# Attention softmax totals: one transfer from SBUF to SBUF instead of a pass through DRAM, and earlier places for the reciprocal and the division

## The chip, the cores and the metric

The kernel runs on one core of a Trainium2 chip. The metric is the time on the device in microseconds (us) of one execution. A core has five engines that run side by side: PE (TensorE, matrix products), DVE (VectorE), ACT (ScalarE), POOL (GpSimd) and SP (SyncE), which in this kernel does nothing but issue transfers. An engine carries out its instructions strictly in the order in which they stand in its queue. If one of them waits, all that stand behind it on that engine wait too. This holds for SP's queue of transfers as well.

## The reference

For four batches of 1024 tokens of width 1024 (float32) the reference computes, cut to what matters:

```
xn  = rms_norm(x) * (1 + scale(emb)) + shift(emb)
q, k, v = split(xn @ W_qkv)              # 16 heads of 64
q, k = rms_norm(q), rms_norm(k)
attn = softmax(q @ k.T / 8)              # 1024 x 1024 for each of 4 x 16 heads
o    = attn @ v
x1   = x + o + o @ W_out
out  = x1 + causal_conv(x1, w = cond, 4 taps) + b
```

The change touches the last step of the softmax: the totals of `exp(...)` over the keys, their reciprocals, and the multiplication of `attn @ v` by them.

## The kernel before, in words

**Units.** The attention of a batch is done for pairs of heads, and for each pair in two halves of 512 queries. That makes 4 x 8 x 2 = 64 units, numbered here 0 to 63 in order of time; units 0 to 15 belong to batch 0. The loop at the end of the kernel makes one turn for each unit p. In turn p TensorE computes the scores of unit p (`scores`, L688) in between the products `attn @ v` of unit p - 1 (`values`, L751, into the one PSUM tile `pav`), then the totals of unit p - 1 (`finish`, L766), and then a long stretch of other products: the projections to q, k and v for later heads (`pqkv`, L648, by a Strassen scheme of seven products), the output projection (`po`, L940 and L1009) and transposes.

**The softmax of a unit.** ScalarE copies the scores to SBUF (L696), VectorE takes a running maximum (`mx`, L705), GpSimd reduces it over the partitions (`mb`, L710), ScalarE copies it to PSUM (`mbp`, L719). Then VectorE subtracts it from eight score tiles (the shifts, L724), ScalarE takes the exponentials (L728) and GpSimd adds them up (`sum`, L730, seven additions one after the other). In the next turn the ones-matrix product L766 adds `sum` over the partitions: the totals.

**The chain from the totals to the division.** `spread` (L784) copies the totals from PSUM to `tots`, where the 4 x 256 totals (two heads, two halves of the queries) lie on partitions 0, 32, 64 and 96. Four transfers write them to DRAM (`scrT`, L787), one reads them back as a tile of 128 partitions by 8 (`few`, L789). `invert` takes the reciprocal of this tile on VectorE (L792), writes it to DRAM (`scrR`, L794) and reads it back twice as broadcast (`rec`, two transfers, L797). `divide` multiplies `pav` by `rec` on VectorE (`oT`, L806) and stores the result (`scrO`, L810). `pav` has one buffer, so the first product of the next unit's `values` waits until `oT` has read it.

**What sets the order.** The orders of PE, DVE, ACT and POOL are written out by hand, by a planner in the kernel. It keeps a clock of its own, in planned microseconds, which is moved by the work that it gives to TensorE (`tick`). `defer(delay, key, step)` puts a step on a list with the due time clock + delay, and at each `tick` all steps that are due are issued in the order of their due times; equal due times go in the order in which they were put on the list. `finish` defers `spread` by 0.2 and `invert` by 8.0. Two `tick`s of 0.9 later `softmax` defers the maximum by 2.6, a filler by 2.7, the shifts by 7.6 + 1.8 per tile (1.6 in batch 0), and the loop defers `divide` by `DIVIDE` = 18.0. The filler (`fill_gap`) issues work on VectorE that has no fixed time: the scaling of q and k (`qk`, L498) and the combinations of weights and of sums (L565, L868, L894). The order of SP's queue is not written by hand: the tile framework places each transfer by its own reckoning of when it can start.

Of the kernel before, what the change touches and what calls it, by code (L numbers as in the profile page):

```python
# [10 lines left out]
F32 = mybir.dt.float32  # L11
# [4 lines left out]
P = 128  # L16
# [5 lines left out]
def kernel(  # L22
# [32 lines left out]
    nc = tc.nc  # L55
# [12 lines left out]
    QN = N // 4  # L68
# [10 lines left out]
    dram = ctx.enter_context(tc.tile_pool(name="dram", bufs=1, space=bass.MemoryType.DRAM))  # L79
# [16 lines left out]
    def defer(delay, key, step):  # L96
        pending.append((clock[0] + delay, next(serial), key, step))
# [10 lines left out]
    def tick(us):  # L108

        clock[0] += us  # L110
        flush(lambda e: e[0] <= clock[0])
# [565 lines left out]
    class Unit:  # L677
# [82 lines left out]
        def finish(self):  # L760
            b, c = self.pr.b, self.pr.c
            tot = ps_m.tile([P, HN], F32, tag="m", name=f"tot_{self.name}")
            for g in range(4):
                h, i = divmod(g, 2)
                some = slice(0, HN) if (b, c) == (B - 1, NJ - 1) else slice(i * QN, (i + 1) * QN)
                nc.tensor.matmul(  # L766
                    tot[32 * g : 32 * (g + 1), : some.stop - some.start],
                    ones,
                    self.sum[:, h, some],
                    start=True,  # L770
                    stop=True,
                )
            tick(2 * PAIR)
            self.tot = tot
            if (b, c) == (B - 1, NJ - 1):
                return
            key = ("tot", self.name)
            defer(0.2, key, lambda: self.spread(tot))
            defer(8.0, key, self.invert)

        def spread(self, tot):

            sums = apool.tile([P, HN], F32, tag="rec", name=f"tots_{self.name}", bufs=1)
            nc.scalar.copy(sums[:, :QN], tot[:, :QN])  # L784
            scr = dram.tile([4, QN], F32, tag=f"tot_{self.name}", name=f"scrT_{self.name}")
            for g in range(4):
                nc.sync.dma_start(scr[g : g + 1, :], sums[32 * g : 32 * g + 1, :QN])  # L787
            self.few = small.tile([P, 2 * HN // P], F32, tag="few", name=f"few_{self.name}", bufs=1)
            nc.sync.dma_start(self.few, scr.rearrange("g (p i) -> (g p) i", p=32))  # L789

        def invert(self):
            nc.vector.reciprocal(self.few, self.few)  # L792
# [280 lines left out]
    SHARES = (0.25, 0.5, 0.25)  # L1073
    LEADS = ((11, 7), (10, 9))
    LEADS_LAST = ((11, 7), (10, 12))
    DIVIDE = 18.0
    STEP_FIRST = 1.6
    BEHIND_FIRST = 22.0
    LATER = ((0, 0), (4, 0))
# [243 lines left out]
    for p in range(B * NB):  # L1323
# [10 lines left out]
        def fill():  # L1334
            run(next(stretches))
# [19 lines left out]
        if last is not None:  # L1355
            defer(2.7 if p > B * NB - 2 else DIVIDE, ("oT", last.pr.b, last.pr.c, last.half), last.divide)
        fill()
# [47 lines left out]
```

## Time and profile before

| | |
|---|---|
| median of 3 runs (2842.89, 2851.01, 2853.53) | 2851.01 us |
| the profiled execution, its own time | 2850.32 us |
| its span, first to last instruction | 2848.5 us |
| busy: PE, DVE, ACT, POOL | 97%, 76%, 54%, 46% |
| PE busy from 160 to 800 us of the span (batch 0) | 605.80 of 640 us |
| PE busy from 800 to 2640 us | 1832.53 of 1840 us |
| PE busy from 2640 us to the end | 191.43 of 209 us |
| mean granted TensorE clock | 0.993 |
| mean busy share of the DMA engines, 160 to 800 us, 800 to 2640 us | 0.52, 0.55 |

A line of the page's list of waits reads: engine and line of the waiting instruction, `<-` what ended its wait, then the total in us, the number of times and the longest. A line of the timeline reads: start in us, length in us, engine, line, operation, tiles `out<-in`, shape, the number of instructions merged, and in brackets the idle time of the engine just before them and what ended it.

### The profile page before, as it was taken

The page shows a single profiled execution, that of the slowest core. Times are in us where ns is not written, and L with a number is a line of the kernel's source. Part 1 is how long each engine was busy: PE and PEld are TensorE (multiplying, and loading weights), DVE is VectorE, ACT ScalarE, POOL GpSimd, SP SyncE. Part 2 cuts the span into 40 slices and gives each one's busy share as a digit, 9 for nine tenths or more (in the row PEclk, how much of TensorE's full clock was granted, in tenths as well). Part 3 has the DMA queues.
Part 4 walks back from the last instruction along what each step waited for, and adds up shares of the span by engine and source line. Part 5 has one row for each costly group of instructions (what it writes and reads, how often), then busy time and mean ns, then how long its engine had stood idle before and what let it go on. Part 6 is the DMA issues. An engine that isn't in the chain of part 4 may idle for free.

```text
span 2848.5 us, 32001 instructions
## 1 busy us (share of the span) xinstructions
PE 2764.3 (97%) x10581; PEld 1315.6 (46%) x10581; DVE 2162.1 (76%) x2579; ACT 1541.5 (54%) x2221; POOL 1323.4 (46%) x534
## 2 busy tenths in 40 slices
PE   6999999999999999999999999999999999999998
PEld 3544444444444445444444445444444444444344
DVE  4578788877888777788777777788778867787863
ACT  4255666655555566655555556565455545555532
POOL 2055554455554454353555355354455445544520
PEclk9999999999999999999999999999999999999999
DMA  9854555645554556674565556665565444533334
GB/s 318 276 170 145 192 174 187 204 152 172 174 196 158 175 192 209 208 234 161 165 208 180 169 180 212 193 228 182 166 214 197 144 135 165 167 104 105 114 108 118
DMA packets 416844, 509.40 MB, mean 179 GB/s; under 512 B 40816, under 2 KB 326824, under 8 KB 406952
## 3 DMA queue, kind: packets, MB, share of 16 engines
q1 hardware_dynamic: 416680, 507.36, 54.6%
q8 instruction: 85, 1.39, 0.2%
q14 instruction: 79, 0.65, 0.1%
HBM read 411.85 MB, written 95.40 MB: 178 GB/s over the span
## 4 chain that ended last, share of the span: by engine, by line
PE 79%; DVE 11%; DMA 4%; ACT 2%; issue 2%; SPq 1%; POOL 0%; DVEq 0%; ACTq 0%; POOLq 0%
PE pqkv_P L648 31%; PE pav L751 16%; PE s L688 15%; PE po L1009 5%; PE po_P L940 5%; DVE mx L705 4%; PE po L940 4%; DVE sp L724 2%; PE qkt L506 1%; DVE qk L498 1%; DMA rec<-scrR 1%; ACT sp L696 1%; PE po L995 1%; PE tot L766 1%; DMA we<-in_L_cond_W_emb_dram 1%
## 5 line engine op out<-in xcount | busy, mean ns | idle before, releaser
L648 PE MATMUL pqkv_P<-w_P,a 128*128 128x384 f32 x3456 | 1177.5, 492 | 18.2 <-issue 6.6
L730 POOL TENSOR_TENSOR sum<-sum,sp 128x1024 f32<-128x1024 f32 x384 | 934.7, 2434 | 35.9 <-ACT sp L728 4.8
L648 PEld LDWEIGHTS pqkv_P<-w_P,a 128*128 128x128 f32 x3456 | 642.4, 191 | 482.7 <-issue 77.7
L696 ACT COPY sp<-s 128x1024 f32<-128x1024 f32 x512 | 501.2, 1017 | 500.1 <-PE s L688 500.0
L728 ACT ACTIVATE sp<-sp 128x1024 f32<-128x1024 f32 x512 | 531.9, 1055 | 221.3 <-DVE sp L724 217.6
L724 DVE TENSOR_TENSOR sp<-sp,mbp 128x1024 f32<-128x1024 f32 x512 | 603.5, 1209 | 21.4 <-ACT mbp L719 21.2
L710 POOL PARTITION_ALL_REDUCE mb<-mx x64 | 219.7, 3432 | 849.7 <-DVE mx L705 421.3
L705 DVE TENSOR_TENSOR mx<-mx,sp 128x1024 f32<-128x1024 f32 x384 | 486.3, 1266 | 133.2 <-ACT sp L696 103.6
L688 PE MATMUL s<-qT,kT 64*128 64x512 f32 x2048 | 509.0, 615 | 2.0 <-ACT sp L696 2.0
L751 PE MATMUL pav<-sp,v 128*64 128x512 f32 x2048 | 484.5, 605 | 17.4 <-DVE oT L806 17.1
L730 POOL TENSOR_TENSOR sum<-sp,sp 128x1024 f32<-128x1024 f32 x64 | 151.5, 2366 | 486.7 <-ACT sp L728 186.5
L688 PEld LDWEIGHTS s<-qT,kT 64*128 64x128 f32 x2048 | 175.6, 185 | 306.3 <-issue 137.6
L751 PEld LDWEIGHTS pav<-sp,v 128*64 128x64 f32 x2048 | 131.6, 137 | 334.5 <-issue 287.4
L1045 DVE SCALAR_TENSOR_TENSOR y<-x,cols,y 128x512 f32<-128x512 f32 x192 | 241.7, 1263 | 48.0 <-ACT y L1033 43.4
L705 DVE TENSOR_TENSOR mx<-sp,sp 128x1024 f32<-128x1024 f32 x64 | 105.2, 1644 | 138.2 <-ACT sp L696 138.2
L667 DVE TENSOR_TENSOR qk<-u,pqkv_P 128x256 f32<-128x256 f32 x256 | 105.7, 413 | 74.0 <-PE pqkv_P L648 73.2
L1009 PE MATMUL po<-ob,wo 128*128 128x512 f32 x352 | 155.4, 593 | 0.5 <-DVE wo L989 0.5
L940 PE MATMUL po_P<-o_P,wq_P 128*128 128x512 f32 x320 | 143.9, 592 | 0.8 <-DMA o_P<-scrS 0.8
L498 DVE TENSOR_TENSOR qk<-qk,ms 128x1024 f32<-128x1024 f32 x64 | 136.0, 2145 | 0.0
L719 ACT COPY mbp<-mb 128x1024 f32<-128x1024 f32 x64 | 65.1, 1017 | 105.6 <-POOL mb L710 105.3
L940 PE MATMUL po<-o_P,wq_P 128*128 128x512 f32 x240 | 108.0, 592 | 0.0
L485 ACT ACTIVATE sq<-qk 128x512 f32<-128x512 f32 x128 | 76.8, 628 | 55.1 <-DVE qk L667 55.1
(94 smaller groups left out, 1753.0 us busy)
## 6 DMA issues: line engine op xcount, KB each, us to landing
a<-scrA SPq DMA_DIRECT2D x212, 512.0 KB
w_P<-scrB SPq DMA_DIRECT2D x64, 768.0 KB
o_P<-scrS SPq DMA_DIRECT2D x40, 1024.0 KB
w_P<-in_L_cond_W_qkv_dram SPq DMA_DIRECT2D x192, 192.0 KB
o_P<-scrO SPq DMA_DIRECT2D x30, 1024.0 KB
scrA<-r SPq DMA_DIRECT2D x28, 896.0 KB
wq_P<-scrW SPq DMA_DIRECT2D x70, 256.0 KB
xc<-in_x_dram SPq DMA_DIRECT2D x64, 256.0 KB
```

The lines of the kernel that those rows point to most:

```text
L648: nc.tensor.matmul(pm, (chunk.r(place) if a is None else a[:, k, :])[:, t % 2 * P : (t % 2 + 1) * P], w[:, k, :], start=(k == 0), stop=(k ...
L688: nc.tensor.matmul(ps[:, h, :], pr.kT[kt // HT][h * D : (h + 1) * D, kt % HT * P : (kt % HT + 1) * P], pr.qT[self.half][h * D : (h + 1) * ...
L696: nc.scalar.copy(sp, ps)
L705: nc.vector.tensor_max(self.mx, self.mx if kt > 1 else self.sp[0], self.sp[kt])
L710: nc.gpsimd.partition_all_reduce(self.mb.rearrange("p h q -> p (h q)"), self.mx.rearrange("p h q -> p (h q)"), P, bass_isa.ReduceOp.max,)
L724: nc.vector.tensor_sub(self.sp[kt], self.sp[kt], self.mb)
L728: nc.scalar.activation(sp, sp, AF.Exp)
L730: nc.gpsimd.tensor_tensor(self.sum, self.sum if kt > 1 else self.sp[0], sp, ALU.add)
L751: nc.tensor.matmul(self.pav[h * D : (h + 1) * D, :], self.pr.v[kt // HT][:, kt % HT, h * D : (h + 1) * D], self.sp[kt][:, h, :], start=(kt ...
L940: nc.tensor.matmul(pm, self.w[name][:, k, :], self.o[name][:, k, :], start=(k == 0 and name not in ("P2", "P3", "P4")), stop=(k == KH - 1),)
L1009: nc.tensor.matmul(self.pm, self.w[kh][:, k % KH, :], oTs[b, k, half], start=False, stop=(k == NJ - 1),)
L1045: nc.vector.scalar_tensor_tensor(self.y, self.x1[:, k : k + HN], cols[:, r : r + 1], self.y, ALU.mult, ALU.add)
```

## The change

The totals go from `tots` to `few` by one transfer of SP that reads four partitions of SBUF and writes 128; the tile `scrT` in DRAM and its four transfers are gone. The delay of `invert` goes from 8.0 to 4.5 planned microseconds, and `DIVIDE` from 18.0 to 12.0. Every unit from 0 to 61 goes through this code. The last two take the reciprocal of the whole totals on VectorE (L804), and the division of unit 62 has a delay of its own.

```diff
             key = ("tot", self.name)
             defer(0.2, key, lambda: self.spread(tot))
-            defer(8.0, key, self.invert)
+            defer(4.5, key, self.invert)
 
         def spread(self, tot):
 
             sums = apool.tile([P, HN], F32, tag="rec", name=f"tots_{self.name}", bufs=1)
             nc.scalar.copy(sums[:, :QN], tot[:, :QN])
-            scr = dram.tile([4, QN], F32, tag=f"tot_{self.name}", name=f"scrT_{self.name}")
-            for g in range(4):
-                nc.sync.dma_start(scr[g : g + 1, :], sums[32 * g : 32 * g + 1, :QN])
             self.few = small.tile([P, 2 * HN // P], F32, tag="few", name=f"few_{self.name}", bufs=1)
-            nc.sync.dma_start(self.few, scr.rearrange("g (p i) -> (g p) i", p=32))
+            nc.sync.dma_start(self.few, sums[0:P:32, :QN].rearrange("g (p i) -> g p i", p=32))
...
-    DIVIDE = 18.0
+    DIVIDE = 12.0
```

## The prediction

> **What bounds the kernel now.** First the windows by stage: PE is busy 1832.53 of 1840 us between 800 and 2640 us, so the change cannot win more than 7.5 us there. The room is in batch 0 (160 to 800 us, 34.2 us idle) and at the end (from 2640 us). Next the list of waits, for what the changed chain costs, on PE, on DVE and in SP's queue:
>
> ```profile
> PE pav L751 <- DVE oT L806: 17.1, 10, 5.1
> ...
> DVE oT L806 <- DMA rec<-scrR: 44.8, 24, 4.2
> ...
> DVE few L792 <- DMA few<-scrT: 11.7, 8, 1.7
> ...
> SPq L787 <- ACT tots L784: 827.3, 61, 18.3
> ...
> SPq L797 <- DMA scrR<-few: 89.7, 41, 4.0
> ```
>
> PE waits ten times for a division. VectorE waits 24 times for `rec`, but only PE's time counts. The timeline of unit 13's division, one of the ten, shows why:
>
> ```profile
> 672.48 0.38 ACT L784 COPY tots<-tot 128x256 f32<-128x256 f32 x1
> ...
> 672.88 1.12 SPq L787 DMA_DIRECT2D scrT<-tots  x4
> 674.87 0.34 SPq L789 DMA_DIRECT2D few<-scrT  x1
> ...
> 682.73 1.03 SPq L794 DMA_DIRECT2D scrR<-few  x1
> ...
> 688.14 1.13 SPq L797 DMA_DIRECT2D rec<-scrR  x2
> ...
> 681.80 0.20 DVE L792 RECIPROCAL few<-few 128x8 f32<-128x8 f32 x1
> ...
> 685.19 2.34 DVE L724 TENSOR_TENSOR sp<-sp,mbp 128x1024 f32<-128x1024 f32 x2
> ...
> 693.52 0.69 DVE L806 TENSOR_TENSOR oT<-pav,rec 128x512 f32<-128x512 f32 x1 [1.54 <-DMA rec<-scrR]
> ...
> 694.27 5.35 PE L751 MATMUL pav<-sp,v 128*64 128x512 f32 x16 [2.14 <-DVE oT L806]
> ```
>
> From here times count from the end of the `tots` copy (672.86 here). `few` is asked for at 2.0, but its reciprocal stands in VectorE's queue behind other work, until 8.9. `scrR` is issued at 9.9, `rec` at 15.3, and the division starts at 20.7, after seven shifts; PE was ready at 19.3. The 16 products after that wait take 5.35 us, against 3.65 us after unit 1's wait of 1.55 us: the profile has the granted clock at half for 3.4 us from 695.0.
>
> **The change part by part.** *The transfers.* Four of about 0.28 us on SP and a pass through DRAM go. Read from the packets: `scrT` lands 1.67 us after the copy in 60 of 62 units (nothing else is then in the queue), and `few`, an equal 128 pieces of 32 bytes, needs 0.26 us once it starts (unit 1: 0.94 to 1.20 after issue). The new transfer, issued at 0.03, should land near 1.6 us. Its price from SBUF to SBUF is not in the trace; bounds are 1.2 (that row without waiting) and 4.2 us (unit 32, 2.8 to 7.0, where `few` queued behind a load). I take 1.6, since the queue is empty. The maximum ends on VectorE at 2.5 us in nearly every unit, so this is covered; at 4.2 VectorE would wait 1.2 us before work whose cover is GpSimd's reduction, until 6.0.
>
> [...]
>
> *The reciprocal, 0.2 us, and the three transfers behind it.* At 4.5 its due time equals that of the filler (1.8 + 2.7). In the planner's floating-point clock it goes first in 55 units (31 exact ties, which its earlier place in the list decides, 24 earlier by rounding) and after the filler in seven, units 4 to 10. In the 55 it moves to about 3.0 us, ahead of the filler's work (675.72 to 681.34 in unit 13, so 5.6 us). Where VectorE waited for `rec`, so that its landing can be read, it came 8 us after the reciprocal with little in the queue (unit 61: 11.4 to 19.3) and 10 to 12 with loads between (unit 13: 8.9 to 20.7): landing at 11 to 15. In the seven the reciprocal gains only 0.4 to 2.5 us and comes at 6 to 9.5, so `rec` lands at 14 to 20. SP's waits at `scrR` and `rec` remain and move forward past loads of `w_P`, `a`, `xg`; these are issued 1 to 4 us later at worst, and PE waits for a load once after 800 us (0.8 us).
>
> *The division, 0.69 us.* Planned 12.0 puts it after the third shift instead of the sixth or seventh, at 11.0 to 15 us. In the 55 units `rec` is there or late by up to 2 us; in the seven VectorE stalls 0 to 6 us. Behind it stand five shifts and the evacuations of projection products. After 800 us those have cover: stalls of 3.0 to 4.2 us (units 17, 21, 33) cost PE nothing there. I price the 55 at nothing.
>
> *What PE gains.* The waits in batch 0 (units 1, 2, 5, 6, 10 to 15) are 17.1 - 5.1 = 12.0 us, all ended by the division; `rec` need only land by 18.6 us (PE ready at 19.3, less the division). The halved clock after unit 13 goes too: 5.35 - 3.65 = 1.7.
>
> *What is late next: GpSimd's additions.* Their end stands before the totals product by 2.4 us in unit 1, 2.7 in unit 5, 1.9 in unit 11, 4.9 in unit 13. An earlier `pav` eats that. It also brings the next maximum under the additions: an addition of 2.36 us takes 3.22 when a `mx` gets in between. Slack less gain less 0.87 leaves -0.3 in unit 11, -0.1 in unit 5, near zero in 1 and 13. Price: 1.0 us. The seven reciprocals behind the filler cost units 5 and 6 part of their gain and a little evacuation in 7 to 9: 1.4 us, bounds 0 and 6 (stalls of 5 us each in 5, 7 and 9, with nothing between).
>
> *The end, unit 61.* The wait of 5.1 us goes, but nothing comes of it:
>
> ```profile
> 2684.46 16.27 POOL L730 TENSOR_TENSOR sum<-sum,sp 128x1024 f32<-128x1024 f32 x6
> ...
> 2685.33 5.17 PE L751 MATMUL pav<-sp,v 128*64 128x512 f32 x16 [5.07 <-DVE oT L806]
> ...
> 2700.78 1.06 PE L766 MATMUL tot<-sum,ones 128*32 128x512 f32 x8 [0.80 <-POOL sum L730]
> ```
>
> The totals already wait for GpSimd, and earlier scores put more maxima between its additions. I take 0, bounds -1.7 (one more stretch at half clock) and +3.7 (0.8 and the later 2.9 us wait for unit 62's division).
>
> *Sum:* 12.0 + 1.7 - 1.0 - 1.4 + 0 = 11.3 us. 2850.3 - 11.3 = 2839.0; the profiled execution lies 0.7 under the median, so 2840.
>
> **The rivals.** *More than the sum.* VectorE's other waits go as well (44.8 us on `rec`), the other idle of batch 0 (34.2 - 12.2 = 22 us, much of it PE waiting for VectorE's evacuations) shrinks, and the end gives its 3.7. With the seven units at no cost and half of a 7 us share: 12.0 + 1.7 + 3.7 + 3.5 = 21 us, 2830. Against it: VectorE has little spare in those stretches, and the division's 0.69 us moves into them.
>
> *The additions take the whole.* If three more maxima get between them (3 x 0.87 = 2.6 us), slack less gain less 2.6 is -11.8 us summed over those units, and 13.7 - 11.8 - 1.4 = 0.5 us remains: 2850, no change. For it: units 15 and 61, with three maxima before the last addition, have a slack of 0.05. Against it: the others have one or two there, and `pav` moves by 1 to 2 us only.
>
> *Slower: `rec` comes late for the earlier division.* If SP's order leaves `scrR` behind bulk loads as now (unit 1: reciprocal 9.1, issue 12.4; unit 21: 6.1, 11.4), `rec` lands at 16 to 20 while the division stands at 13.5. VectorE then stalls 3 to 6 us in some 30 units, in mid-stretch, where each PSUM evacuation behind it is needed within two or three projection products of 2.58 us. It decides from a stall of about 5 us, two such products, beyond the rows of up to 4.2 that cost nothing; a stall of 5.65 us costs PE 0.65, and in 30 units, with nothing won in batch 0, that is +19.5: 2870. Against it: with the reciprocal 3 to 6 us earlier, `scrR` is ready before most of those loads.
>
> *That the change does not do what it says:* only in the seven units, as priced.
>
> **How the numbers follow.** Forecast 0.45: own range 4 to 18 us, 2833 to 2847, of which 0.17 lies past the bound of 14.3 us (0.5%, about what a measurement of this kernel can tell from no change). More than the sum 0.27, all past it. Additions 0.06. Late `rec` 0.22, nearly all past 0.5% on the other side. So faster 0.17 + 0.27 = 0.44, same 0.28 + 0.06 = 0.34, slower 0.22. The range for 8 in 10 takes in most of the first rival and the nearer half of the last: 2825 to 2862.
>
> **What would show it.** Right: the wait `pav` on `oT` gone in batch 0; reciprocals near 3 us, `rec` issued before 8; GpSimd at the totals instead. Wrong: waits of `oT` on `rec` grown past 100 us with PE idle at L648 behind them, or a reciprocal that waits for `few` in most units; or new PE waits for loads, if moving SP's waits holds them back.

## The result, and the profile after

| | before | after |
|---|---|---|
| median | 2851.01 us | 2863.11 us (2859.76 to 2865.95) |
| ratio, after to before | | 1.0047, 95% interval 1.0029 to 1.0066 |
| the profiled execution, its own time and span | 2850.32, 2848.5 us | 2859.76, 2858.0 us |
| mean granted TensorE clock | 0.993 | 0.993 |
| PE idle between the totals of unit 0 and of unit 16 | 32.7 us | 40.3 us |
| the same, ended by a division | 12.2 us | 0 us |
| time from the totals of unit 0 to those of unit 16 | 608.6 us | 617.0 us |
| units 16 to 61 | 1878.0 us | 1881.9 us |
| totals of unit 61 to the end of the span | 183.4 us | 185.7 us |

2840 us was forecast, with 2825 to 2862 as the range; the change made the kernel about 13 us slower. The last rows of the table are read from the ends of the `tots` copies in the two traces. The stretch ahead of unit 0, which the change does not touch, took 178.6 us in the one execution and 173.4 us in the other, so the two spans differ by less than the three stretches do. A stretch of a single execution also moves by itself: the kernel with the transfer alone, which below is as fast as the kernel before, has 612.5 us between units 0 and 16 in its profile, 3.9 more.

The list of waits of the changed kernel, in the same columns as before, has these lines where the prediction showed those of before:

```profile
DVE oT L803 <- DMA rec<-scrR: 27.4, 13, 5.1
...
PE tot L766 <- POOL sum L730: 9.1, 4, 7.5
...
PE xtp L312 <- ACT qT L514: 8.1, 2, 6.0
PE xtp L312 <- DVE ou L956: 7.0, 2, 3.6
...
PE pav L751 <- DVE oT L803: 1.8, 1, 1.8
...
SPq L786 <- ACT tots L784: 863.3, 62, 18.3
...
SPq L794 <- DMA scrR<-few: 42.6, 27, 3.2
```

PE's ten waits for a division have shrunk to one, at unit 61. VectorE's waits for `rec` fell from 44.8 to 27.4 us, and no reciprocal waits for `few` at all. By these lines the chain got shorter, as it was meant to. Three other lines stand where there was little: PE waits for GpSimd's additions (1.2 us before), for `qT` (2.0 us before) and for an evacuation at L956 (2.5 us before, where the line is L959). An evacuation is an instruction of VectorE or ScalarE that reads a product out of PSUM and so makes room for the next one.

The windows by stage of the changed kernel (length, then busy us of PE, PEld, DVE, ACT and POOL with the instructions in brackets, the granted clock, DMA share, GB/s):

```profile
160.00:800.00 640.00, 598.40 (x2334) 278.52 (x2330) 516.99 (x610) 372.64 (x512) 343.56 (x133) 0.99 0.52 168
800.00:2640.00 1840.00, 1829.04 (x7003) 869.76 (x7004) 1435.32 (x1670) 1030.17 (x1456) 894.53 (x352) 1.00 0.55 178
```

PE is busy 7.4 us less than before in batch 0 (605.80) and 3.5 us less in the long stretch after it (1832.53).

The timeline of unit 13, where the prediction had read the old chain:

```profile
677.56 0.38 ACT L784 COPY tots<-tot 128x256 f32<-128x256 f32 x1
677.96 0.60 SPq L786 DMA_DIRECT2D few<-tots  x1
681.21 0.20 DVE L789 RECIPROCAL few<-few 128x8 f32<-128x8 f32 x1
...
683.52 1.17 SPq L794 DMA_DIRECT2D rec<-scrR  x2
...
691.81 0.68 DVE L803 TENSOR_TENSOR oT<-pav,rec 128x512 f32<-128x512 f32 x1
...
696.29 2.82 PE L648 MATMUL pqkv_P<-w_P,a 128*128 128x384 f32 x8 [1.25 <-issue]
...
699.04 3.22 PE L751 MATMUL pav<-sp,v 128*64 128x512 f32 x14
```

From the end of the copy (677.94): reciprocal at 3.3, `rec` issued at 5.6, division at 13.9 without a wait, in place of 8.9, 15.3 and 20.7. The products L751 no longer wait for it. They start at 21.1 all the same, against 21.4 before, because the projection products ahead of them now wait, among others for 1.25 us in which the profile shows nothing that they waited for. This unit won 2.0 us in all, most of it as the stretch at half clock that it no longer has (3.41 us from 695.0 in the kernel before, where it cost 5.35 - 3.65 = 1.7).

### The profile page after: what moved, and what is told of

It reads as the page before. It is cut to its first block, busy times and chain, and to the rows that moved or that the text cites. A ratio compares the mean times of both kernels' runs of the same rounds, so it can differ in the third digit from the quotient of the medians.

```text
span 2858.0 us, 31707 instructions
## 1 busy us (share of the span) xinstructions
PE 2761.6 (97%) x10581; PEld 1313.9 (46%) x10581; DVE 2169.3 (76%) x2579; ACT 1544.3 (54%) x2221; POOL 1328.9 (46%) x534
## 4 chain that ended last, share of the span: by engine, by line
PE 77%; DVE 11%; DMA 5%; ACT 2%; issue 2%; POOL 1%; SPq 1%; DVEq 0%; ACTq 0%; POOLq 0%
PE pqkv_P L648 32%; PE pav L751 14%; PE s L688 14%; PE po L1006 5%; DVE mx L705 4%; PE po_P L937 4%; PE po L937 4%; DVE sp L724 2%; PE qkt L506 2%; POOL sum L730 1%; DMA rec<-scrR 1%; ACT sp L696 1%; PE tot L766 1%; DVE qk L498 1%; PE po L992 1%
## 5 line engine op out<-in xcount | busy, mean ns | idle before, releaser
L705 DVE TENSOR_TENSOR mx<-mx,sp 128x1024 f32<-128x1024 f32 x384 | 499.0, 1299 | 127.8 <-ACT sp L696 96.7
L751 PE MATMUL pav<-sp,v 128*64 128x512 f32 x2048 | 481.3, 602 | 1.8 <-DVE oT L803 1.8
L751 PEld LDWEIGHTS pav<-sp,v 128*64 128x64 f32 x2048 | 130.2, 136 | 316.3 <-issue 291.9
L705 DVE TENSOR_TENSOR mx<-sp,sp 128x1024 f32<-128x1024 f32 x64 | 107.4, 1678 | 150.5 <-ACT sp L696 150.5
L667 DVE TENSOR_TENSOR qk<-u,pqkv_P 128x256 f32<-128x256 f32 x256 | 105.9, 414 | 71.5 <-PE pqkv_P L648 71.1
```

Source lines behind the costliest of these rows:

```text
L705: nc.vector.tensor_max(self.mx, self.mx if kt > 1 else self.sp[0], self.sp[kt])
L751: nc.tensor.matmul(self.pav[h * D : (h + 1) * D, :], self.pr.v[kt // HT][:, kt % HT, h * D : (h + 1) * D], self.sp[kt][:, h, :], start=(kt ...
```

## The experiments

The kernels are written as edits of the changed kernel, except where another is named. All were timed in several rounds against the kernel before on the same chip. That kernel's own median was 2847.26 us beside the first four, 2845.42 beside the next four and 2848.12 beside the last four, so ratios are what can be compared; 0.1% is 2.85 us.

| kernel | reciprocal | division | median, us | ratio to before, 95% interval |
|---|---|---|---|---|
| transfer alone | 8.0 | 18.0 | 2846.45 | 0.9997 [0.9989, 1.0006] |
| transfer and reciprocal | 4.5 | 18.0 | 2847.52 | 0.9999 [0.9989, 1.0008] |
| transfer and division | 8.0 | 12.0 | 3041.52 | 1.0688 [1.0667, 1.0709] |
| reciprocal ahead of the filler everywhere | 4.4 | 12.0 | 2856.34 | 1.0031 [1.0018, 1.0044] |
| before, division without `rec` | 8.0 | 18.0 | 2843.82 | 0.9991 [0.9982, 1.0000] |
| after, division without `rec` | 4.5 | 12.0 | 2849.87 | 1.0015 [1.0006, 1.0024] |
| early in batch 0 alone | 4.4 | 12.0, then 18.0 | 2847.52 | 1.0007 [0.9999, 1.0016] |
| early from batch 1 alone | 4.4 | 18.0, then 12.0 | 2855.31 | 1.0041 [1.0029, 1.0054] |
| units 4 to 10 ahead of the filler | 4.5, seven at 4.4 | 12.0 | 2855.82 | 1.0028 [1.0019, 1.0037] |
| the same, three divisions back | 4.5, seven at 4.4 | 12.0, three at 18.0 | 2849.18 | 1.0008 [0.9998, 1.0017] |
| early, through DRAM | 4.5 | 12.0 | 2891.31 | 1.0153 [1.0138, 1.0167] |
| reciprocal first, division late | 4.4 | 18.0 | 2850.05 | 1.0004 [0.9995, 1.0013] |

### Which of the three edits costs

Two theories stood against each other: that the division's early place costs the time, and that the new transfer or SP's order does. Three kernels undo one edit or two.

```diff
# transfer alone
-            defer(4.5, key, self.invert)
+            defer(8.0, key, self.invert)
-    DIVIDE = 12.0
+    DIVIDE = 18.0
# transfer and reciprocal
-    DIVIDE = 12.0
+    DIVIDE = 18.0
# transfer and division
-            defer(4.5, key, self.invert)
+            defer(8.0, key, self.invert)
```

> The changed kernel with both delays put back (8.0 and 18.0): the single transfer alone. Theory 'place of the division' (the change loses because the division stands in the middle of the shifts, where PSUM evacuations wait behind it): nothing of that is left, and the reciprocals that waited for few (11.7 us on VectorE) go: 2846 to 2852 us. Theory 'transfer' (the SBUF to SBUF transfer or the new order of SP's queue costs): about as slow as the change, 2860 us or more.

> The transfer and the earlier reciprocal (4.5), the division back at 18.0. 'Place of the division': rec lands before 15 us, so the division waits for rec almost nowhere (44.8 us of VectorE waiting go, of which TensorE sees 1.0, 1.3, 1.8, 1.1, 1.5 and 1.8 us in units 1, 5, 11, 12, 13 and 15, 2.0 in unit 61, and 1.7 of halved clock): 2841 to 2847 us, the fastest of these four. 'Transfer': 2860 us or more.

> The transfer and the earlier division (12.0), the reciprocal back at 8.0. 'Place of the division': the reciprocal stands at 6 to 9 us again, rec lands at 15 to 20, and the division stands at 11 to 15: VectorE waits 2 to 6 us in the middle of the shifts in some 40 units (over 120 us on rec), slower than the change: 2875 to 2900 us. 'Transfer': no slower than the change, 2860 to 2866 us.

The transfer alone changes nothing that can be measured, and with the earlier reciprocal it still changes nothing. The loss comes with the division's place. The second kernel was expected to be the fastest, 2841 to 2847, and ended half a microsecond above that, with a ratio of 0.9999. Its trace has no wait of a division for `rec` any more, and these waits of PE:

```profile
PE pav L751 <- DVE oT L803: 3.7, 3, 1.3
PE pqkv_P L648 <- DMA a<-scrA: 3.0, 2, 2.4
...
PE tot L766 <- POOL sum L730: 2.1, 4, 0.8
```

The wait for divisions went from 17.1 to 3.7 us. PE's idle time from the totals of unit 0 to those of unit 16 is 32.9 us, against 32.7 before: what was won there is waited for elsewhere in the same stretch.

The third kernel, which was expected at 2875 to 2900, came to 3042 us. The direction was right and the size far off. Its waits:

```profile
DVE oT L803 <- DMA rec<-scrR: 195.3, 44, 9.6
PE pqkv_P L648 <- DVE v L667: 70.0, 17, 6.5
```

Here the division stands ahead of the landing of its `rec`. VectorE waits 44 times, 4.4 us in the mean, PE waits behind it for the evacuation at L667, and the granted clock falls from 0.993 to 0.971. This is the prediction's slower rival in full size: unit 31 took 51.9 us instead of 42.4, with a wait of 7.6 us on VectorE. Part of the price is the clock: in the profiled execution PE spent 173 us at half clock instead of 37, which by itself is worth about 68 us as an estimate (half of the difference, as unit 13 of the kernel before lost 1.7 us in its 3.4 at half clock).

### What the waits for `rec` were worth

If the first term of the prediction was right, a kernel in which no division ever waits for `rec` must be 12 us or more faster than before. In units 0 to 61 the division is made to multiply by a column of ones, at the old place in the one kernel and at the new place in the other; the chain of transfers is still issued, and the quotient by the totals is left out of the output.

```diff
-            nc.vector.tensor_mul(oT, self.pav, self.rec)
+            by = self.rec if (b, c) == (B - 1, NJ - 1) else ones[:, 0:1].to_broadcast([P, HN])
+            nc.vector.tensor_mul(oT, self.pav, by)
```

> The kernel before, with the division of units 0 to 61 multiplying pav by a column of ones in place of rec: same place, same shape, the whole chain of transfers is still issued, but VectorE never waits for rec. The quotient by the totals is left out of the output of those units. Theory 'PE's waits for the division are PE's time' (the prediction's first term): the 17.1 us of waits and the halved clock behind them go, 12 to 17 us faster than before, 2830 to 2836. Theory 'batch 0 is bound by the rest of VectorE's and GpSimd's work': the waits of pav on oT go, others take their place in the same turns, at most 4 us, 2843 to 2848, and PE's idle time from unit 0 to unit 16 stays near 32 us.

> The changed kernel (reciprocal 4.5, division 12.0) with the same replacement of rec by ones in units 0 to 61, so that the division has its early place and no wait for rec; the quotient by the totals is left out of the output of those units. Theory 'late rec costs the time': the loss against before goes, 2843 to 2850. Theory 'the place itself costs (0.69 us of VectorE ahead of evacuations, and products of attn @ v that bring the maxima forward under the additions)': half or more of the loss stays, 2853 to 2860.

In the kernel before, all 24 waits for `rec` taken away give 0.09%, 2.6 us with an interval from 0 to 5. PE's waits for a division are not all gone there (7.8 us of 17.1 are left, since the division keeps its place); in the second kernel above they were down to 3.7 us, and it won 0.3 us. So the prediction's 12.0 + 1.7 us were not there to be won. The window of batch 0 of the kernel before without `rec` shows it too:

```profile
160.00:800.00 640.00, 607.15 (x2353) 284.00 (x2350) 529.62 (x618) 376.81 (x518) 346.48 (x135) 0.99 0.52 172
```

PE is busy 607.15 us there, 1.35 more than before. Of the idle time between units 0 and 16 the divisions now end 4.9 us instead of 12.2, but the total is 30.8 instead of 32.7: PE's waits for the evacuations `u` of VectorE grew from 2.9 to 6.9 us, and those that the profile shows no cause for ("issue") from 4.1 to 5.4.

In the changed kernel the same edit leaves 0.15%, 4.3 us, of the 13.4. The expectation of the first theory was 2843 to 2850, of the second 2853 to 2860, and 2849.87 is at the upper edge of the first. So `rec` that comes late seems to be the larger part of the loss, about 9 us (1.0047 less 1.0015, with an interval of some 3 to 15 us). The early place by itself also costs: of the two kernels without `rec`, timed side by side, the one with the early place is about 6 us slower (2849.87 against 2843.82), and their intervals do not meet.

### Where the loss lies

```diff
# reciprocal ahead of the filler everywhere
-            defer(4.5, key, self.invert)
+            defer(4.4, key, self.invert)
# early in batch 0 alone: the same, and
-            defer(2.7 if p > B * NB - 2 else DIVIDE, ("oT", last.pr.b, last.pr.c, last.half), last.divide)
+            defer(2.7 if p > B * NB - 2 else DIVIDE if p <= NB else 18.0, ("oT", last.pr.b, last.pr.c, last.half), last.divide)
# early from batch 1 alone: the same 4.4, and
+            defer(2.7 if p > B * NB - 2 else DIVIDE if NB < p < B * NB - 2 else 18.0, ("oT", last.pr.b, last.pr.c, last.half), last.divide)
```

> The whole change with 4.4 in place of 4.5, so that the reciprocal stands before the filler's work in the units 3 to 10 too, where the changed profile has it at 6 to 10 us and loses 11.5 us. 'Place of the division', late rec being the price: those units lose 1 to 4 us in place of 11.5, and units 24 and 40 stay as they are: 2853 to 2857 us. If it is the division's own 0.69 us in the stretch and not rec: 2861 to 2865 us, as the change.

> Reciprocal at 4.4 (ahead of the filler in every unit), division at 12.0 in units 0 to 15 and at 18.0 in the rest. If what is left of the loss in that kernel with 12.0 everywhere (9 us, of which its profiled execution has 5.7 between the totals of units 0 and 16, 2.4 between units 16 and 61) lies where its profile shows it: 4 to 7 us over before, 2851 to 2854, with halved clock in batch 0 of 17 us or more. If batch 0 gains by the earlier division and the loss is later: 2838 to 2846.

> The complement: reciprocal at 4.4, division at 18.0 in units 0 to 15 and in unit 61, at 12.0 in units 16 to 60. By the profile of the kernel with 12.0 everywhere: 2 to 4 us over before, 2849 to 2851, the waits in the turns after units 24 and 40 (about 3 us each, for an evacuation at L956 that stands behind the division) still there. By the other reading, that batches 1 to 3 carry the loss: 2854 to 2858.

The first was expected at 2853 to 2857 and came to 2856.34; its waits for `rec` are down to 5.8 us. The two halves were a miss. From the profile of the first I had put the larger part of the rest into batch 0, 4 to 7 us, and 2 to 4 us behind it. Measured are +0.07% in batch 0, no difference that can be told, and +0.41%, 11.7 us with an interval from 8 to 15, from batch 1 on. With a `rec` that is in time the early division costs nothing that can be told in batch 0; the loss lies behind it. How much exactly stays open: the halves add to more than the 9 us of the whole, within their intervals, and the profiled execution of the second half has 7.7 us of its loss between units 0 and 16, where only the transfer and the reciprocal's place differ from before. Unit 61 has its late division in both halves.

The place in that long stretch can be read from the turns. Of units 17 to 59 only units 24 and 40 are over 1 us longer in the changed kernel, by 1.7 and 2.9 us. Unit 24 there, and then in the kernel before:

```profile
1118.33 0.38 ACT L784 COPY tots<-tot 128x256 f32<-128x256 f32 x1
...
1121.12 3.41 DVE L326 TENSOR_TENSOR r<-r 128x256 f32<-128x256 f32 x4
...
1124.45 0.19 DVE L789 RECIPROCAL few<-few 128x8 f32<-128x8 f32 x1
...
1134.27 0.69 DVE L803 TENSOR_TENSOR oT<-pav,rec 128x512 f32<-128x512 f32 x1 [1.42 <-DMA rec<-scrR]
1134.88 0.68 DVE L953 TENSOR_TENSOR x<-ou,po_P 128x512 f32<-128x512 f32 x1
1135.47 0.68 DVE L956 TENSOR_TENSOR ou<-ou,po_P 128x512 f32<-128x512 f32 x1
...
1136.21 0.66 PE L312 MATMUL xtp<-ident,xg 128*128 128x128 f32 x4 [3.37 <-DVE ou L956]
```

```profile
1129.47 0.68 DVE L959 TENSOR_TENSOR ou<-ou,po_P 128x512 f32<-128x512 f32 x1
...
1130.20 0.66 PE L312 MATMUL xtp<-ident,xg 128*128 128x128 f32 x4 [1.26 <-DVE ou L959]
...
1136.41 0.68 DVE L806 TENSOR_TENSOR oT<-pav,rec 128x512 f32<-128x512 f32 x1
```

The division with its wait, 1.42 + 0.69 us, stands ahead of two evacuations, and a transpose of PE waits for the second. In the kernel before the division stood 7 us behind them, and the same transpose waited 1.26 us. The difference, 2.1 us, is the wait and the division, 2.11 us, with no cover at all. The `rec` is late because the reciprocal stands behind four instructions at L326 (3.41 us) and comes 5.7 us after the copy. Unit 40 shows the same waits (its division waits 1.65 us, the transpose 3.60), and 6.8 us at half clock in place of 3.4. The profile of the kernel before has 3.4 us at half clock in each of the two turns; the one of the transfer alone has the same waits of PE there and none, and its two turns are 1.7 us shorter. Beside that execution the changed kernel loses 3.4 and 4.6 us in them.

In batch 0 the largest single loss is unit 9, one of the seven in which the reciprocal stands behind the filler:

```profile
528.09 0.19 DVE L789 RECIPROCAL few<-few 128x8 f32<-128x8 f32 x1
528.67 0.45 SPq L791 DMA_DIRECT2D scrR<-few  x1
...
533.55 1.30 SPq L794 DMA_DIRECT2D rec<-scrR  x2
...
539.85 0.69 DVE L803 TENSOR_TENSOR oT<-pav,rec 128x512 f32<-128x512 f32 x1 [5.10 <-DMA rec<-scrR]
...
541.70 1.06 ACT L728 ACTIVATE sp<-sp 128x1024 f32<-128x1024 f32 x1 [4.80 <-DVE sp L724]
542.66 0.57 ACT L514 COPY qT<-qkt 128x512 f32<-128x512 f32 x1
...
543.28 1.11 PE L312 MATMUL xtp<-ident,xg 128*128 128x128 f32 x4 [6.01 <-ACT qT L514]
```

From the copy's end at 519.7 the reciprocal comes at 8.4 and `rec` is issued at 13.9; the division stands at 15.0 and waits until 20.1. The next shift stands behind it, ScalarE's exponential waits 4.80 us for that shift, and the evacuation that PE needs next, the copy `qT`, stands behind the exponential on ScalarE. PE idles 6.01 us. The unit is 5.3 us longer.

Two kernels put these readings to the test one after the other: the reciprocal of the seven units alone goes ahead of the filler, and then the divisions of units 24, 40 and 61 go back to their old place.

```diff
+        unit.p = p
-            defer(4.5, key, self.invert)
+            defer(4.4 if 4 <= self.p <= 10 else 4.5, key, self.invert)
# and, in the second kernel only
-            defer(2.7 if p > B * NB - 2 else DIVIDE, ("oT", last.pr.b, last.pr.c, last.half), last.divide)
+            defer(2.7 if p > B * NB - 2 else 18.0 if last.p in (24, 40, 61) else DIVIDE, ("oT", last.pr.b, last.pr.c, last.half), last.divide)
```

> The changed kernel with the reciprocal of units 4 to 10 alone at 4.4, so that it stands ahead of the filler there too; all other units as in the changed kernel (4.5, division 12.0). If the seven units behind the filler cost what their turns show in the changed kernel's profile (units 4 to 10 together +9.5 us against before, of which unit 9 has 5.3): 3 to 7 us over before, against 13 for the change. If their loss is the division's place, not the late rec: 9 to 14 us over before.

> The same, and in units 24, 40 and 61 the division goes back to 18.0. If the rest of the loss is the division ahead of the evacuation at L956 in units 24 and 40 (1.7 and 2.9 us longer in the changed kernel's profile) and the later totals at the end (2.4 us): within 2 us of before. If it is spread over the other units: no change against the kernel without this step.

The first step brings the loss from 0.47% to 0.28%, a gain of 5.4 us; it ended at 8.0 us over before, a little above the 3 to 7 expected, and unit 9 is back at its old length. The intervals of the two ratios meet, so the size is known only roughly, and the step by itself is not clear of nothing. In the profiled execution, the slowest of its eleven (2860.13 us), PE idles 35.0 us between units 0 and 16 instead of 40.3, but has 27.3 us at half clock instead of 13.7, and the stretch is as long as in the changed kernel. The second step, on the same chip, brings 1.0028 to 1.0008, 5.7 us, with intervals that do not meet. The lines behind it:

```profile
PE tot L766 <- POOL sum L730: 6.3, 4, 3.6
...
PE xtp L312 <- DVE ou L956: 2.5, 2, 1.3
```

The waits at L956 are those of before again (2.5 us; 7.0 in the kernel without this step), and the longest wait for GpSimd's additions, 6.3 us at unit 61 without it, is 1.8 there. In the two profiles the turns after units 24 and 40 are 3.8 and 3.0 us shorter and the end 0.8; the three divisions were not put back one by one. Together seven reciprocals and three divisions out of 62 hold some 11 of the 13 us (1.0047 less 1.0008, with an interval of about 5 to 17 us). The 0.08% that remain can't be told from nothing.

### Whether the single transfer is needed

```diff
# the kernel before
-            defer(8.0, key, self.invert)
+            defer(4.5, key, self.invert)
-    DIVIDE = 18.0
+    DIVIDE = 12.0
```

> The kernel before with both delays of the change (reciprocal 4.5, division 12.0) but the totals still through DRAM. By the trace of before few lands 3 to 4 us after the copy, and 4 to 7 where a load stands in front of it, while the reciprocal now stands at 2.4 to 4: if that wait costs, VectorE's waits for few grow from 11.7 us to 50 or more and the time is 18 to 30 us over before, so that the single transfer is what makes the early reciprocal possible. If VectorE's work behind it has room: 10 to 15 us over before, as the change.

```profile
DVE few L792 <- DMA few<-scrT: 109.2, 51, 4.4
```

The way through DRAM costs 1.5% at the new places, 44 us, more than the 18 to 30 expected, and some 30 us more than the change. VectorE waits 51 times for `few`, which lands 5.0 us after the copy in the median of before's packets, and 44.1 us more for `rec`. The single transfer does what it says; the old kernel only had no use for it.

### Whether an early reciprocal costs by itself

In the profiles of the kernels with 4.4 GpSimd's additions were late in the turns after units 0 and 4.

> One transfer, reciprocal at 4.4 in every unit, division at 18.0 in every unit. If the reciprocal's place itself costs in batch 0 (in the three kernels with 4.4 the first addition of GpSimd in the turns after units 0 and 4 comes 3 to 4 us after its operands, and PE waits 2 to 4 us at the totals): 3 to 7 us over before with those waits. If it costs only together with an early division: within 2 us of before.

2850.05 us, ratio 1.0004: no difference. The waits are in its profile (3.86 us at the totals after unit 0, 1.96 us after unit 4), and no loss shows in the time, so the same waits in the profiles above must not be read as the price of the change.

## Why the prediction was wrong

*The transfer: right.* By the packets (128 of 32 bytes in every unit) `few` landed 1.53 to 1.62 us after the copy; 1.6 was taken. Its packets took 0.29 us from first to last, about as those of the read from DRAM in unit 1 of the kernel before (0.26).

*The reciprocals and the order: right but for five units.* In the seven units 4 to 10 the reciprocal stood behind the filler, at 6 to 9.8 us, and in 50 others it came at 2.4 to 4.1. Units 3, 24, 40, 60 and 61, at 5.7 to 6.7, were counted among those that come near 3 us; in units 24 and 40 this made `rec` late.

*What PE gains, 12.0 and 1.7 us: the step that failed.* The waits did go, and the time did not. The sum counted each wait of PE that a division ended as PE's time, and subtracted what "is late next" for GpSimd's additions only, 1.0 us. What was late next differs with the kernel: without `rec`, VectorE's evacuations `u` of the projection products (6.9 us instead of 2.9); with the early reciprocal alone, a load of `a` (3.0 us), a shift (2.5 us) and smaller waits. The kernel without any wait for `rec` puts the whole term at 2.6 us; the one with one transfer and an early reciprocal at 0.3. The half clock after unit 13 went as foreseen, but between units 0 and 16 the changed kernel has 13.7 us at half clock, the kernel before 10.2, and the one with the transfer alone 17.1; such a sum differs by the execution.

That PE's idle time in batch 0 stays between 31 and 35 us in the profiles of all kernels but three (the change, the early division with the late reciprocal, and the early places through DRAM) is shown. What it is bound by there was not tested; VectorE's busy share of 81% (516.99 of 640 us in the changed kernel) and the evacuations named above speak for its queue, but that is an argument only.

*The seven units, 1.4 us, with bounds 0 and 6: mis-sized.* They measured about 5.4 us, near the upper bound, with an interval that reaches 0. The bound's own case, a stall of 5 us with nothing between, is what happened in unit 9, once.

*The 55 units at nothing: wrong in two of them.* "Stalls of 3.0 to 4.2 us (units 17, 21, 33) cost PE nothing" is true of those units, and of 41 of the 43 units from 17 to 59. It was taken for all of them. Units 24 and 40 have an evacuation that PE already waited for in the kernel before, 1.26 us each, so its list of waits held the two places with no cover; the new place of the division was never laid beside it.

*The end at 0, bounds -1.7 and +3.7: within the bounds.* It cost 2.3 us in this pair of executions. The wait for the division went from 5.1 to 1.8 us, and the one for GpSimd's additions from 0.8 to 7.5, which the list of things to look for had named in kind:

```profile
2693.04 18.14 POOL L730 TENSOR_TENSOR sum<-sum,sp 128x1024 f32<-128x1024 f32 x6
...
2711.23 1.94 PE L766 MATMUL tot<-sum,ones 128*32 128x512 f32 x8 [7.52 <-POOL sum L730]
```

The six additions took 18.14 us instead of 16.27: earlier scores brought the next maxima between them.

*The slower rival* had the right mechanism, VectorE held in mid-stretch by `rec`. It expected stalls of 3 to 6 us in some 30 units; the changed kernel has 13 waits for `rec`, the longest of 5.1 us, and what it lost lies, as far as the profiles show, above all in one such stall, two short ones at bare places and the end. The point from which a stall was to cost, about 5 us, holds for unit 9, but stalls of 1.42 and 1.65 us cost as well at the bare places. The price, 0.65 us of PE's time for a stall of 5.65, was far too low: in the kernel with the division ahead of a late `rec`, 195.3 us of VectorE's waits go with a loss of 196 us (6.88% of 2847), about a third of it by the clock (the estimate of 68 us above).

## What to carry to other kernels

An engine's wait is worth its length only if nothing else would end that wait a moment later: before it is booked as a gain, make the awaited thing free in a kernel that still does all the other work, and read the time. For a step that moves forward on an in-order queue, lay its new place beside the list of waits of the engine that matters: every wait that is ended there by an instruction which the step now precedes has no cover, and can pay the whole of the step and its own wait (2.11 us in unit 24 here). Ten units of 62 made most of the result here, so a price that is right for the typical turn must be asked again for the few that differ.

## What the runs showed of the hardware

The four source partitions of the new transfer cost it nothing that shows: its 128 packets run from 1.26 to 1.55 us after the copy in the median of 62 units, 0.29 us, where the read of 128 equal pieces from DRAM took 0.26 us in unit 1 of the kernel before.

A halved clock did not need a long wait here. In the kernel before it followed a single wait of 2.14 us (unit 13, from 695.0 us) as well as two of 1.63 and 1.19 us that began 3.3 us apart (unit 7, from 452.7 us); a wait of 2.05 us in the same trace, from 489.1 us, had none behind it. Between 160 and 2840 us each such stretch lasted 3.41 us in the kernel before, and 3.41 or 6.83 us in the changed one. What decides whether a wait is followed by one was not shown. Nearly the same idle time in batch 0 went with 10.2 us at half clock in the kernel before (32.7 us idle) and with 23.9 in the kernel with 4.4 and 12.0 (33.2 us idle). With half of the difference counted as lost, as in unit 13, that is about 7 us, an estimate.

A maximum (`mx`, L705) and an addition of GpSimd that met mostly both took longer: at the changed kernel's end four maxima took 2.20 us and three times 3.17 to 3.18, where one that started just ahead of an addition took 1.23, and the additions beside them 3.20 to 3.41 instead of 2.37. One after the other a pair would take about 3.6 us as an estimate (2.37 + 1.23); the rows show one pair every 3.3 us.

Not explained is the first addition of a unit, which often starts later than its operands are ready. In the turn after unit 0 of the kernel that divides early from batch 1 on, the second exponential ended at 186.3 and the addition started 4.1 us later:

```profile
190.46 2.37 POOL L730 TENSOR_TENSOR sum<-sp,sp 128x1024 f32<-128x1024 f32 x1 [10.45 <-ACT sp L728]
```

In the kernel before the same lag was 0.5 us there and up to 3.4 us in other units. The row names an exponential as what ended the wait; the fourth ended 0.3 us before the addition, which reads the first two alone. Shifts and evacuations ran back to back on VectorE in that span; whether they hold the addition was not tried.
